# A MetaFormer block on one core: the whole convolution stage in 64x64 tensor tiles, in two rounds over pairs of PSUM banks

## The chip, the core and the metric

The kernel runs on one core of one Trainium2 chip. The metric is the device time of one execution in microseconds (us). The kernel before was run three times: 953.1, 950.99 and 952.64 us, median 952.64. One further execution was taken by the hardware profiler. PE is TensorE (the matrix engine; PEld are its weight loads), DVE is VectorE, ACT is ScalarE, POOL is GpSimd, SP is SyncE, which issues most transfers here.

## What is computed

The input is `x` of shape 4 x 32 x 128 x 128 in float32: 4 batches and 32 tokens (channels), each an image of 128 x 128. Two layers follow one another:

```python
x = x + _L0_conv_ref(_ln_c(x), ...)      # spectral attention and mixers
t = x as tokens; t = t + _L0_ffn_ref(_ln_t(t), W, V, gamma, beta)
x = x + _L1_conv_ref(_ln_c(x), bias, up_filter, dn_filter)
t = x as tokens; t = t + _L1_ffn_ref(_ln_t(t), W, V, gamma, beta)
```

`_ln_c` and `_ln_t` normalise each row of 128 numbers. The part that concerns us is the second convolution and the two neighbours of it:

```python
def _L1_conv_ref(x, bias, up_filter, dn_filter):
    x = x + bias                                    # one number per token
    x = repeat(repeat(x, 2, axis=2), 2, axis=3)     # 128x128 -> 256x256
    x = _conv_same(x, up_filter)                    # 12x12, separable
    x = leaky_relu(x, 0.2) * sqrt(2)
    x = _conv_same(x, dn_filter)                    # 12x12, separable
    return x[:, :, ::2, ::2]                        # back to 128x128

def _L1_ffn_ref(x, W, V, gamma, beta):
    Wx = einsum('bti,hi->bth', x, W)                # product of the features
    Wx = batch-normalised over all rows, times gamma plus beta
    y_t = sigmoid(wx_t + y_{t-1} @ V.T)             # a scan over tokens and rows
    return ys
```

The scan runs over all tokens and rows, `32 * 128` steps in sequence for each batch.

## The kernel before, in words

The whole activation, `XA` (128 partitions, 4 batches, 32 tokens, 128 columns), stays in SBUF. The program has these stages: the attention (to about 235 us in the profile), the mixers, whose order of work is the hand-set list `MIXERS` (to about 487 us), the first scan (to 547 us), **the convolution stage (547 to 869 us)**, and the second scan with the output (869 us to the end). The scans take all tokens and batches side by side, in four pieces of 32 rows each, which start from a guess with 12 rows of run-up and are checked at the end; `WX` holds the products before a scan and the states after it. If a check fails, a slow sequential program would run after it; it does not here.

The convolution stage is one function body, `parallel()`, from line 1980 on. Its order of work is the list `CONVOLUTIONS` (lines 54 to 117), some 1,500 pieces that a planner wrote out beforehand. `in_order` (line 499) ties the instructions of PE, DVE, ACT, POOL and, in this stage, SP to the order in which the pieces are issued, so each engine does its share of the list strictly in sequence. A piece is a letter code and a number: a token `t` (0 to 31) or a unit `u` (0 to 63; one unit is one token and two of its four batches). For one token the pieces are:

- `Y t` (lines 1961 and 2057): four 128x128 transposes on PE turn the states of the first scan back to rows, into a PSUM tile `ps_y`; `A t` (line 2060) adds them to `XA` on DVE.
- `CS`, `CN`, `CP`, `CO`: row statistics of the sum (DVE, line 383), means and variances by seven small DVE operations (lines 370 and 2004), the power -1/2 on POOL (line 2016), shifts on DVE (line 2019). Groups of one to four tokens share them.
- `X t.b` (line 2065): the normalised image `XN` of one batch. For b = 3 ACT makes it, else POOL; the first two tokens use DVE and ACT.
- `Ra u`, `Rb u` (line 2101): the row half of the upsampling filter, two batches, as matmuls with 64 rows and 128 columns of weights and 134 moving columns; `Q u` (line 2118) copies the result to `q1` on ACT.
- `Ka u`, `Kb u` (line 2123): the column half, the same tile shape, into two single-bank PSUM tiles.
- `La`, `Lb` (line 2141): ACT writes `above = relu(0.8 x)` from PSUM; `Va`, `Vb` (line 2147): DVE writes `U = 0.2 x + above`, reading the same PSUM bank and `above`.
- `Da v`, `Db v` (line 2155): both halves of the downsampling filter, of unit `v` and of unit `v - 1`, as 64x64 matmuls with 67 moving columns; `C`, `E` copy the results on ACT, `AD` adds to `XA` on DVE.
- `FS`, `FN`, `FP`, `FO`, `N`: the statistics of the result, and the normalised features `xn` (two batches on POOL, two on ACT); `FS` also issues from SP the transfer of the token's rows to DRAM.
- `T t` (line 427): four 128x128 transposes; `TC` copies them on ACT; `M t` (line 441): one 128x128 matmul over 512 columns; `PS` (DVE) takes its statistics and `PC` (ACT) puts it into `WX`.

A float32 matmul appears in the profile as two matmuls and two weight loads, a transpose as one of each.

[...]two row tiles with different data can run side by side[...]. That is why `R`, `K` and `D` come in two rounds, a and b: in round a the upper row tile writes the bank of batch 0 and the lower one that of batch 1, in round b they change places and add to what is there. Round b may begin only when round a is through, which the program ensures by an empty instruction on SP that waits for round a and for which round b waits (lines 2045 to 2055). Before, those empty instructions wait for the first matmul of each tile in round a by their code.

[...]Before, the pool `ps_t` (line 1873) has four single-bank buffers that `Y`, `K`, `T`, `M`, and later the output share; the pool `ps_c1` (line 1984) has two banks for `R` and two for `D`.

Of the kernel before, what the change touches and what calls it, by code (L numbers as in the profile page):

```python
# [54 lines left out]
Y0 Y2 A0 Y1 A2 Y3 Y4 CS0 Y5 A1 CN0 Y6 CS1 CP0 CS2 CO0 CN1 X0.0 CP1 A3 X0.1 X0.3 X0.2 Ra0 CS3 Y7 Rb0 CO1 A4 Q0 X1.0  # L55
Ra1 CN2 X1.3 Y8 X1.1 X1.2 Rb1 CP2 CS4 Q1 A6 Ra2 A5 Rb2 CO2 Ka0 CS5 X2.0 X3.0 Kb0 X2.3 CS6 X2.2 X3.3 X3.2 Q2 CK X2.1
Lb0 Ra3 X3.1 La0 Rb3 Va0 A7 Vb0 Y9 CS7 Da0 A8 Db0 CN3 C0 Ka1 CS8 Y10 CP3 Kb1 A10 La1 A9 Lb1 Va1 Q3 Y11 CS9 Ra5 Y14
CO3 Rb5 Vb1 X4.0 A11 X4.3 X4.1 Da1 X4.2 CS10 Ka2 CS11 Db1 A14 Kb2 C1 CN4 La2 Ka3 E0 Va2 Lb2 CP4 Kb3 Q5 AD0 Y12 Vb2
La3 Ra4 A12 Da2 Lb3 Va3 Rb4 CS12 Db2 Q4 X5.0 X5.3 X5.2 CO4 Ka4 C2 X5.1 Ra6 Vb3 Kb4 E1 CS14 Ka5 La4 Da3 Lb4 AD1 Va4
Rb6 FS0 Db3 Vb4 Kb5 C3 Y15 La5 Y13 E2 A15 Q6 Da4 Va5 Lb5 Ra7 AD2 Db4 Vb5 A13 Ka6 C4 CS15 Rb7 E3 Kb6 X8.0 Q7 AD3 Da5  # L60
La6 X8.2 CS13 X8.1 Lb6 Ka7 Va6 X8.3 Ra8 Db5 FS1 Kb7 C5 Vb6 Rb8 La7 CN5 Y16 E4 Y19 Lb7 Va7 CP5 Da6 Q8 AD4 Vb7 Ra9 Db6
A16 A19 Ka8 C6 Rb9 CS16 E5 Kb8 X6.0 Q9 CO5 Da7 X6.2 X6.3 AD5 X6.1 La8 Ra10 CS19 Ka9 Lb8 Db7 Va8 FS2 Kb9 C7 Rb10 La9
Vb8 Y17 E6 Va9 Q10 Da8 Lb9 AD6 A17 Ka10 Db8 Vb9 CS17 Kb10 C8 Ra11 La10 Y18 E7 Va10 Rb11 Lb10 Da9 X7.0 Q11 AD7 Vb10
X7.1 X7.3 Ka11 X7.2 FS3 Ra12 Db9 A18 Rb12 C9 FN0 Kb11 Q12 Y20 CS18 FP0 E8 La11 Ra13 Da10 AD8 Lb11 Va11 Rb13 A20 Ka12
Q13 Vb11 Db10 CN6 Kb12 C10 FO0 Ka13 CS20 CP6 La12 Ra14 E9 Kb13 Va12 Lb12 Da11 AD9 La13 Vb12 Rb14 FS4 Db11 Q14 Lb13
N1.0 CO6 Ka14 C11 N0.0 Ra15 Va13 N1.1 N1.2 Kb14 E10 N0.1 Rb15 Vb13 La14 Da12 Q15 AD10 Lb14 Ka15 N1.3 Db12 N0.3 N0.2
Ra16 Va14 C12 Kb15 E11 T0 Vb14 La15 Da13 AD11 TC0 FS5 Lb15 Rb16 Db13 Q16 Ra17 C13 Va15 T1 E12 Vb15 Rb17 N2.0 TC1
Da14 X9.0 AD12 Q17 X10.0 X9.3 Ka16 X9.1 N2.2 Ka17 X10.1 X10.3 Kb16 X9.2 N2.3 Db14 La16 X11.0 X10.2 Lb16 Ra18 Va16
X11.1 Kb17 C14 X11.2 X11.3 M0 Vb16 N2.1 E13 La17 N3.0 AD13 Da15 Lb17 PS0 N3.1 N3.3 FS6 Rb18 N3.2 Db15 Q18 PC0 T2
Va17 C15 Ra19 Vb17 M1 TC2 E14 AD14 Da16 PC1 PS1 Ka18 Db16 Kb18 C16 Rb19 La18 M2 X12.0 E15 Va18 Q19 X12.1 Da17 Lb18  # L70
X12.2 AD15 PS2 X12.3 Ka19 Vb18 Ra20 PC2 Kb19 FS7 Db17 La19 Lb19 FN1 Rb20 C17 T3 Va19 FP1 Q20 Y21 E16 Vb19 Ra21 TC3
Da18 AD16 A21 Ka20 CS21 Db18 FO1 Kb20 C18 N4.0 Rb21 N5.0 La20 M3 X13.0 E17 Va20 Lb20 N4.1 Da19 Q21 X13.2 AD17 Vb20
X13.3 X13.1 Ka21 N4.3 N5.1 FS8 Ra22 N4.2 Kb21 PC3 Db19 La21 PS3 Lb21 Rb22 Va21 C19 T4 Y22 Q22 Vb21 N7.0 Y24 E18 N7.1
TC4 A22 Da20 N5.3 AD18 N5.2 CS22 Ka22 N7.2 Ra23 N7.3 A24 Kb22 Db20 La22 CS24 Lb22 Rb23 Va22 C20 T5 X14.0 Q23 M4 Vb22
N6.0 E19 X14.2 TC5 AD19 Da21 X14.1 N6.2 PS4 N6.1 N6.3 Ka23 FS9 X14.3 Ra24 PC4 Kb23 Db21 La23 Lb23 Rb24 Va23 C21 T6
Q24 M5 Vb23 E20 TC6 AD20 Da22 PC5 Ka24 PS5 Ra25 Db22 Kb24 C22 Rb25 La24 M6 X15.0 E21 Va24 Q25 X15.1 Da23 Lb24 X15.2
AD21 PS6 X15.3 Ka25 Vb24 Ra26 PC6 Db23 FS10 Kb25 C23 Rb26 La25 T7 E22 Y23 Va25 Q26 Da24 Lb25 AD22 A23 TC7 Ra27 Vb25
Db24 CS23 Ka26 C24 Rb27 CN7 E23 Kb26 X16.0 Q27 Da25 X16.1 AD23 La26 CP7 FS11 Lb26 Ka27 X16.3 Ra28 Va26 Db25 FN2 Kb27
C25 Vb26 Rb28 La27 M7 E24 FP2 CO7 Q28 Da26 Va27 Lb27 PC7 AD24 Ka28 Vb27 Ra29 Kb28 PS7 Rb29 La28 X16.2 Db26 FO2 Lb28
X17.0 Y25 Q29 N9.0 Va28 Y26 X17.2 C26 A25 X17.1 Ra30 X17.3 Vb28 Y27 N8.0 E25 N9.2 N9.1 Da27 AD25 N8.2 N8.1 A26 N9.3  # L80
Ka29 N8.3 FS12 Db27 CS25 Kb29 C27 A27 Rb30 La29 T9 CS26 E26 T8 Lb29 N10.0 Da28 TC9 N11.0 Va29 N10.1 TC8 AD26 N11.1
Db28 Vb29 Q30 N10.3 CS27 Ka30 C28 Ra31 N11.3 Kb30 CN8 E27 N11.2 Da29 AD27 CP8 La30 FS13 Lb30 M8 N10.2 Va30 Rb31 PC8
Db29 Vb30 Q31 PS8 C29 Ka31 X18.0 CO8 Ra32 E28 X18.1 Kb31 X18.3 AD28 X18.2 Da30 La31 Lb31 Va31 Rb32 Db30 Q32 Vb31
Ka32 C30 Ra33 E29 Kb32 AD29 Da31 La32 FS14 Lb32 Rb33 Va32 M9 Q33 X19.0 X19.3 X19.2 Vb32 Ka33 PC9 X19.1 Ra34 PS9 Db31
Kb33 C31 Rb34 La33 T10 E30 T11 Va33 Q34 Da32 TC10 AD30 Lb33 Ra35 TC11 Db32 Vb33 C32 Ka34 Rb35 E31 Kb34 X20.0 Q35
AD31 Da33 La34 X20.2 FS15 X20.1 Lb34 Ka35 Va34 X20.3 Ra36 Kb35 FN3 M10 La35 Vb34 FP3 Rb36 Lb35 PS10 Db33 Q36 PC10
Ra37 Va35 C33 M11 Vb35 E32 PC11 Da34 AD32 FO3 N12.0 PS11 Ka36 N13.0 N12.2 Db34 N12.1 N12.3 N13.1 N13.3 Kb36 C34 Rb37
La36 T12 X21.0 E33 Y28 Va36 N14.0 X21.3 Da35 X21.2 Q37 AD33 X21.1 TC12 A28 Ra38 N14.1 Lb36 FS16 M12 N14.3 N14.2 Vb36
Rb38 PC12 Db35 CS28 Q38 N13.2 Ka37 PS12 C35 Ra40 Kb37 E34 Ka38 La37 AD34 Da36 Lb37 Va37 Kb38 Vb37 Db36 La38 Lb38
Rb40 Va38 C36 T14 Q40 T13 Vb38 E35 N15.0 Ra39 TC13 AD35 Da37 N15.1 TC14 FS17 N15.2 Rb39 Ka40 N15.3 X22.0 Q39 Db37  # L90
X22.1 X22.3 X22.2 Ka39 C37 Ra41 E36 Kb39 AD36 Da38 La39 Lb39 Va39 Kb40 Db38 La40 Vb39 Rb41 C38 Va40 X23.0 Q41 M13
X23.2 E37 X23.3 X23.1 AD37 Lb40 Da39 PS13 Vb40 Ra42 PC13 Db39 FS18 Ka41 C39 Rb42 E38 Kb41 Q42 AD38 Da40 La41 Lb41
Ka42 Va41 Ra43 Kb42 Vb41 Db40 La42 Lb42 Rb43 Va42 C40 M14 X24.0 Q43 Vb42 X24.2 T15 E39 X24.1 PS14 X24.3 Da41 TC15
AD39 PC14 Ka43 FS19 Ra44 Kb43 FN4 Db41 Lb43 FP4 La43 Rb44 C41 M15 Va43 Q44 Y29 Vb43 E40 PC15 Da42 AD40 A29 Ka44 FO4
PS15 Ra45 N16.0 Kb44 N17.0 CS29 N16.2 Rb45 N16.1 La44 Db42 X25.0 Q45 N17.1 Y30 Va44 C42 X25.1 Ra46 X25.3 A30 X25.2
Ka45 E41 Lb44 AD41 Da43 N16.3 CS30 N17.2 Kb45 N17.3 Vb44 Db43 La45 FS20 Lb45 Rb46 T16 C43 Va45 T17 Q46 N18.0 Vb45
Y31 E42 N19.0 TC16 Da44 AD42 N18.1 N19.2 A31 N19.1 N18.3 Ka46 TC17 CS31 Ra47 Kb46 N19.3 N18.2 Rb47 CN9 Db44 La46
X26.0 Lb46 CP9 M16 Va46 C44 Q47 Vb46 M17 E43 X26.3 PS16 Da45 PC17 AD43 PC16 FS21 Ra48 X26.1 Db45 X26.2 CO9 Rb48 C45
PS17 Ka47 Q48 T18 E44 Kb47 TC18 AD44 Da46 La47 Lb47 Va47 Ra49 Db46 Vb47 Ka48 C46 Rb49 E45 Kb48 X27.0 Q49 AD45 Da47
X27.2 La48 FS22 X27.1 X27.3 Ka49 Lb48 Va48 Ra50 Kb49 Vb48 Db47 La49 Lb49 Rb50 Va49 C47 M18 Q50 Vb49 T19 E46 PS18  # L100
Da48 TC19 AD46 PC18 Ka50 Ra51 Kb50 Db48 La50 Lb50 Rb51 Va50 C48 M19 X28.0 Q51 Vb50 X28.1 E47 X28.2 Ra52 PS19 X28.3
Da49 AD47 PC19 Rb52 FS23 Ka51 Q52 Db49 FN5 Kb51 C49 FP5 Ka52 La51 Ra53 E48 Kb52 Va51 Lb51 Da50 AD48 La52 Vb51 Rb53
# [172 lines left out]
def _network(  # L275
# [1585 lines left out]
    def parallel():  # L1861
# [20 lines left out]
        class Recurrence(Inputs):  # L1882
# [98 lines left out]
        with (  # L1981
# [75 lines left out]
            def state_rows(t):  # L2057
                ps_y[t] = f0.rows(t)
# [300 lines left out]
```

## Time and profile before

| what | value |
|---|---|
| median of three runs | 952.64 us (950.99 to 953.1) |
| the profiled execution | 953.73 us, of which the span is 951.6 us |
| PE busy, whole span | 846.8 us (89%) |
| DVE, ACT, POOL busy, whole span | 741.7, 662.7, 243.3 us |
| convolution stage, 547 to 869 us | 322.0 us |
| PE busy in it | 309.2 us, 8012 matmuls |
| DVE, ACT, POOL busy in it | 231.5, 227.9, 118.8 us |

The span runs from the first to the last instruction of the profile. The busy times of an engine are the union of its instructions, so neighbours that overlap in the pipeline count once. Matmul ends are modelled, so their starts are the better guide. In a group's line the first number is busy time, then the mean length of one instruction, then the idle time ahead of it and what ended that.

### The profile page before, as it was taken

The numbers are of one execution on the slowest core, as the hardware profiler recorded it, in microseconds if no ns is written. First come the engines' busy times: TensorE is split into PE (matmuls) and PEld (weight loads), VectorE is DVE, ScalarE is ACT, GpSimd is POOL, SyncE is SP. The second block draws the span as 40 slices with busy tenths as digits, with TensorE's granted clock in tenths as the row PEclk, the third lists the DMA queues.
The fourth block names the chain that finished last, engine by engine and source line by source line (L and its number), as shares of the span: only waits on it lengthen the run. The fifth ranks groups of instructions, "written<-read, shape, count | busy, mean of one in ns | idle before, by whom it ended". The sixth has DMA issues, their size and how long they took to land.

```text
span 951.6 us, 30245 instructions
## 1 busy us (share of the span) xinstructions
PE 846.8 (89%) x12310; PEld 620.9 (65%) x12310; DVE 741.7 (78%) x2381; ACT 662.7 (70%) x1640; POOL 243.3 (26%) x448
## 2 busy tenths in 40 slices
PE   2999979997897889997879969999999999997995
PEld 2666556677565555644357857888787888775884
DVE  5997477876668899899888888967676576667997
ACT  2775546667745878989778824687777777776773
POOL 2000000020244545355310033443353244131000
PEclk9999979996777999999999969999999999998998
DMA  9905000000101111120000000110110101117443
GB/s 227 222 4 118 1 1 1 1 1 1 46 23 31 39 46 46 46 68 26 20 1 1 1 1 14 38 37 26 37 37 26 37 26 37 37 38 265 162 165 133
DMA packets 69013, 49.60 MB, mean 52 GB/s; under 512 B 4417, under 2 KB 63809, under 8 KB 68801
## 3 DMA queue, kind: packets, MB, share of 16 engines
q1 hardware_dynamic: 68529, 47.31, 17.3%
q8 instruction: 99, 1.62, 0.7%
q0 software_dynamic: 288, 0.01, 0.2%
q10 hardware_dynamic: 48, 0.26, 0.2%
q14 instruction: 49, 0.40, 0.1%
HBM read 30.68 MB, written 16.88 MB: 50 GB/s over the span
## 4 chain that ended last, share of the span: by engine, by line
PE 55%; DVE 23%; ACT 6%; issue 2%; POOL 2%; DVEq 0%; ACTq 0%; SPq 0%; POOLq 0%
PE ps_dn L2162 11%; PE ps_up L2131 8%; PE ps_scan L1911 8%; PE ps_up L2108 4%; DVE XA L1582 4%; PE ps_wx L444 3%; DVE XA L1581 3%; PE ps_y L1301 3%; PE pm L1053 2%; PE ps_inv L479 2%; PE ps_st L1424 2%; DVE ps_scan L1912 2%; PE ps_xt L430 2%; DVE bn L447 2%; PE ps_out L2230 1%
## 5 line engine op out<-in xcount | busy, mean ns | idle before, releaser
L2151 DVE SCALAR_TENSOR_TENSOR U<-ps_up,above 128x512 f32<-128x512 f32 x128 | 85.0, 685 | 51.9 <-ACT above L2144 33.1
L1912 DVE SCALAR_TENSOR_TENSOR ps_scan<-WXY,bs,ps_scan 128x128 f32<-128x128 f32 x352 | 102.2, 361 | 11.3 <-PE ps_scan L1911 9.5
L2162 PE MATMUL ps_dn<-WXY,U 64*64 64x67 f32 x4096 | 90.6, 226 | 1.0 <-ACT p L2191 0.5
L2131 PE MATMUL ps_up<-WXY,q 64*128 64x134 f32 x1024 | 91.1, 299 | 0.4
L2162 PEld LDWEIGHTS ps_dn<-WXY,U 64*64 64x64 f32 x4096 | 72.5, 134 | 28.3 <-ACT p L2191 10.4
L2144 ACT ACTIVATE above<-ps_up 128x512 f32<-128x512 f32 x128 | 73.3, 602 | 20.9 <-PE ps_up L2131 19.1
L444 PE MATMUL ps_wx<-xt,wvt 128*128 128x512 f32 x128 | 70.5, 637 | 6.5 <-ACT WXY L451 4.5
L2131 PEld LDWEIGHTS ps_up<-WXY,q 64*128 64x128 f32 x1024 | 68.7, 189 | 9.3 <-ACT q L2121 1.2
L2036 POOL TENSOR_SCALAR XN<-XA,c_r,c_o 128x128 f32<-128x128 f32 x90 | 42.9, 487 | 99.7 <-PE ps_up L2108 71.1
L2187 ACT COPY q<-ps_dn 128x512 f32<-128x512 f32 x64 | 37.7, 589 | 44.0 <-PE ps_dn L2162 43.8
L2108 PE MATMUL ps_up<-WXY,XN 64*128 64x134 f32 x512 | 60.3, 313 | 6.9 <-DVE XN L2036 3.4
L848 PE MATMUL ps_st<-cst,XA 128*128 128x130 f32 x256 | 43.4, 309 | 14.8 <-ACT XA L831 11.6
L1639 ACT ACTIVATE xn<-XA,f_o,f_r 128x128 f32<-128x128 f32 x120 | 50.9, 489 | 4.7 <-DVE f_o L1621 4.6
L447 DVE BATCH_NORM_STATS2 bn<-ps_wx 128x6 f32<-128x512 f32 x64 | 44.2, 694 | 12.2 <-ACT WXY L451 8.2
L1418 ACT ACTIVATE Z<-Z,k,aB 128x128 f32<-128x128 f32 x128 | 51.0, 480 | 3.4 <-DVE Z L1413 3.2
L848 PEld LDWEIGHTS ps_st<-cst,XA 128*128 128x128 f32 x256 | 35.1, 205 | 27.9 <-ACT XA L831 12.7
L2162 PE MATMUL ps_dn<-WXY,q 64*64 64x67 f32 x2048 | 53.0, 218 | 0.0
L2108 PEld LDWEIGHTS ps_up<-WXY,XN 64*128 64x128 f32 x512 | 40.5, 192 | 18.2 <-issue 5.4
L1581 DVE SCALAR_TENSOR_TENSOR XA<-ps_inv,r1B,xin 128x128 f32<-128x128 f32 x128 | 44.1, 345 | 8.7 <-PE ps_inv L1574 8.7
L1582 DVE SCALAR_TENSOR_TENSOR XA<-Z,gB,XA 128x128 f32<-128x128 f32 x128 | 46.5, 363 | 5.0
L451 ACT COPY WXY<-ps_wx 128x512 f32<-128x512 f32 x60 | 35.0, 587 | 21.9 <-DVE bn L447 16.8
L430 PEld LDWEIGHTS ps_xt<-ident,xn 128*128 128x128 f32 x256 | 28.7, 142 | 29.6 <-ACT xt L438 7.5
(443 smaller groups left out, 2155.9 us busy)
## 6 DMA issues: line engine op xcount, KB each, us to landing
XA<-in_x_dram SPq DMA_DIRECT2D x16, 512.0 KB, 7.3
xin<-in_x_dram SPq DMA_DIRECT2D x32, 256.0 KB, 3.2
turned<-XA SPq DMA_DIRECT2D x32, 256.0 KB, 2.3
XA<-turned SPq DMA_DIRECT2D x8, 1024.0 KB, 14.4
out_dram<-res SPq DMA_DIRECT2D x64, 128.0 KB, 2.1
WXY<-dd SPq DMA_DIRECT2D x4, 544.0 KB, 11.1
WXY<-md SPq DMA_DIRECT2D x4, 144.0 KB, 5.5
WXY<-m1d SPq DMA_DIRECT2D x1, 544.0 KB, 11.5
```

Source lines behind the costliest of these rows:

```text
L444: mm(self.held[t], self.t[:, 0, :], xt, start=True, stop=True)
L447: nc.vector.bn_stats(self.stats[:, t, :], self.held[t].rearrange("p b w -> p (b w)"))
L848: mm(p[:, i, :], XA[:, b, t0 + j + i, :], cst[:, C_E : C_E + 130], start=True, stop=True)
L1581: stt(a, p2[c, b][:, i], r1B[:, j : j + 1], xin[c, b - b % 2][:, b % 2, i], ALU.mult, ALU.add)
L1582: stt(a, Z[c][:, b, i], gB[c][:, n : n + 1], a, ALU.mult, ALU.add)
L1911: mm(p4, self.t[:, 1, :], prev, start=True, stop=True)
L1912: stt(p4, WX[:, :, h, :], s[:, 0:1], p4, ALU.mult, ALU.add)
L2108: i = mm(dst[:, :, reach[k]], XN[u // 2][h, u % 2 * H2 + b, :], UR[h, :, reach[k]], start=(n == 0), stop=(n == 1), skip_group_check=True)
L2131: i = mm(dst[:, r, :, reach[k]], q1[u][w, b, r * P : r * P + P], UC[w, :, reach[k]], start=(n == 0 and r == 0), stop=(n == 1), skip_group_ ...
L2144: nc.scalar.activation(above[u, k], pu[u][k], AF.Relu, scale=1.0 - SLOPE)
L2151: stt(U[u][:, k].rearrange("p r s m -> p (r s m)"), pu[u][k], SLOPE, above.pop((u, k)), ALU.mult, ALU.add)
L2162: i = mm(dst, data, taps, start=(n == 0 and (k, j) in new), stop=(n == 1), skip_group_check=True)
```

## The change

All PE work of the convolution stage is written as 64x64 tiles, four at a time, in two rounds over a pair of banks by one helper, `in_rounds`. `Y` and `T` become matmuls against a 64x64 piece of the identity (so they have rounds a and b, and 16 matmuls of 64 columns instead of four transposes of 128), `M` becomes eight matmuls of 256 columns, `R` and `K` have twice as many matmuls, with 64 weight columns each; `D` keeps its matmuls. The empty SP instruction now waits for the last matmul of each tile in round a.

```diff
+            HALVES = slice(0, HALF), slice(HALF, P)
+            REACH = slice(P - E, P), slice(0, E)
+            TILES = [(i, j) for i in range(2) for j in range(2)]
...
+            def in_rounds(name, pool, products):
+                def piece(n):
+                    def run(u):
+                        if n == 0:
+                            banks[name, u] = pool.tile([P, 2, 4 * P], F32, tag="x", name=f"ps_{name}")
+                        last = {}
+                        for i, j, dst, data, taps in products(u, banks[name, u], n):
+                            m = mm(dst, data, taps, start=(n == 0 and (i, j) not in last), stop=(n == 1),
+                                   skip_group_check=True)
+                            if n == 1 and (i, j) not in last:
+                                after(m, ended[name, u])
+                            last[i, j] = m
+                        if n == 0:
+                            ended[name, u] = nc.sync.nop(nofuse=True)
+                            for m in last.values():
+                                after(ended[name, u], m)
+                    return run
+                return piece(0), piece(1)
...
+            def turned_by(source):
+                def products(t, p, n):
+                    for c in range(2):
+                        for i, j in TILES:
+                            b = i ^ n
+                            o = c * P + i * HALF
+                            yield (i, j, wide(p, b)[HALVES[j], o : o + HALF],
+                                   source(t, HALVES[i], 2 * b + c, HALVES[j]), ident[HALVES[i], HALVES[i]])
+                return products
...
+            def feature_products(t, p, n):
+                for i, j in TILES:
+                    b = i ^ n
+                    yield (i, j, wide(p, b)[HALVES[j]], f1.t[HALVES[i], 0, HALVES[j]],
+                           xt[t][HALVES[i], 2 * b : 2 * b + 2, :].rearrange("p b h -> p (b h)"))
...
+            def up_cols(u, p, n):
+                for r in range(2):
+                    for i, j in TILES:
+                        b = i ^ n
+                        o = r * P + j * HALF
+                        dst = p[:, b].rearrange("p (r s m) -> p r s m", r=2, s=2)
+                        yield (i, j, dst[HALVES[j], r, :, REACH[i]], q1[u][HALVES[i], b, o : o + HALF],
+                               UC[HALVES[i], :, REACH[i]])
```

The leaky ReLU changes sides. ACT now copies the raw sum out of PSUM, and DVE works from SBUF alone:

```diff
-                    above[u, k] = cv.tile([P, 4 * P], F32, tag="above", name="above")
-                    nc.scalar.activation(above[u, k], pu[u][k], AF.Relu, scale=1.0 - SLOPE)
+                    raw[u, k] = cv.tile([P, 4 * P], F32, tag="raw", name="raw")
+                    nc.scalar.copy(raw[u, k], banks["k", u][:, k])
...
-                    stt(U[u][:, k].rearrange("p r s m -> p (r s m)"), pu[u][k], SLOPE, above.pop((u, k)),
-                        ALU.mult, ALU.add)
+                    v = raw.pop((u, k))
+                    stt(U[u][:, k].rearrange("p r s m -> p (r s m)"), v, SLOPE, v, ALU.mult, ALU.max)
```

POOL takes over the image of batch 3 of the convolution's input and of batch 2 of the features from ACT, and the means take six small DVE operations instead of seven:

```diff
-                normalise(("DVE", "ACT", "DVE", "ACT")[b] if t < 2 else "ACT" if b == 3 else "POOL",
+                normalise(("DVE", "ACT", "DVE", "ACT")[b] if t < 2 else "POOL",
...
-                normalise(("DVE", "DVE", "ACT", "ACT")[b] if t >= NT - 2 else "POOL" if b < 2 else "ACT",
+                normalise(("DVE", "DVE", "ACT", "ACT")[b] if t >= NT - 2 else "POOL" if b < 3 else "ACT",
```

The PSUM pools are cut anew: two banks that `R` and `T` share, two for `D`, and two pairs for `Y`, `M` and `K`. `ps_t` is opened only for the output, with two buffers instead of four, and the weights of the second FFN are turned in a pool of their own between the first scan and the stage, no longer ahead of the scan:

```diff
-        ps_t = ctx.enter_context(tc.tile_pool(name="ps_t", bufs=4, space=PSUM))
...
-        f1 = Recurrence(1, xtp, wk, ps_t, ps_t, ("t", "t"))
-        f1.prepare()
+        with tc.tile_pool(name="ps_f", bufs=1, space=PSUM) as ps_f:
+            f1 = Recurrence(1, xtp, wk, ps_f, ps_f)
+            f1.prepare()
...
-            tc.tile_pool(name="ps_c1", bufs=1, space=PSUM) as ps_c1,
+            tc.tile_pool(name="ps_r", bufs=1, space=PSUM) as ps_r,
+            tc.tile_pool(name="ps_d", bufs=1, space=PSUM) as ps_d,
+            tc.tile_pool(name="ps_k", bufs=2, space=PSUM) as ps_k,
...
-        with tc.tile_pool(name="outp", bufs=3) as outp:
+        with (
+            tc.tile_pool(name="outp", bufs=3) as outp,
+            tc.tile_pool(name="ps_t", bufs=2, space=PSUM) as ps_t,
+        ):
```

Last, the list `CONVOLUTIONS` is written anew for these pieces. A stretch of it, before and after:

```diff
-Q24 M5 Vb23 E20 TC6 AD20 Da22 PC5 Ka24 PS5 Ra25 Db22 Kb24 C22 Rb25 La24 M6 X15.0 E21 Va24 Q25 X15.1 Da23 Lb24 X15.2
...
+Ka24 N7.0 TC4 Db22 Vb23 N7.1 N7.3 Ra25 N7.2 C22 Ma4 Rb25 E21 Kb24 X15.0 Q25 AD21 Da23 Lb24 X15.2 FS10 Mb4 X15.1 La24
```

In the new order 235 of the 289 pairs of rounds have more than one short pass of PE work between a and b, 41 have one short pass (one round of `R`, `T` or `Y`) and 13 have none. Outside this stage the instructions of every engine stand in the same order as before.

## Prediction

> **What bounds the kernel now.** I read the chain of work that ended last first: PE holds over half of it, and its largest lines are the convolution stage's.
>
> ```profile
> PE 55%; DVE 23%; ACT 6%; issue 2%; POOL 2%; DVEq 0%; ACTq 0%; SPq 0%; POOLq 0%
> ```
>
> Then the busy time of each engine by windows, over the whole stage and in parts (the columns are window, length, PE, weight loads, DVE, ACT, POOL with counts, PE clock, DMA share, GB/s).
>
> ```profile
> 547.00:570.00 23.00, 15.64 (x95) 11.46 (x95) 19.97 (x81) 6.42 (x15) 7.72 (x9) 0.70 0.00 1
> 570.00:590.00 20.00, 18.55 (x452) 15.53 (x456) 18.56 (x72) 8.94 (x18) 8.49 (x8) 0.92 0.01 3
> ...
> 715.00:734.00 19.00, 19.00 (x474) 14.52 (x478) 11.90 (x35) 15.78 (x34) 8.61 (x13) 1.00 0.10 28
> ...
> 547.00:869.00 322.00, 309.24 (x8012) 247.17 (x8010) 231.54 (x723) 227.85 (x486) 118.76 (x170) 0.97 0.12 35
> ```
>
> From 590 us on PE is never idle; in the first 43 us DVE is nearly full and PE waits for it. So the stage is PE's, with a head that is DVE's. Busy is not yet useful; what PE's time goes into, its timeline tells (start, length, line, count).
>
> ```profile
> 700.57 0.41 PE L2162 MATMUL ps_dn<-WXY,q 64*64 64x67 f32 x16
> 700.91 0.73 PE L2131 MATMUL ps_up<-WXY,q 64*128 64x134 f32 x8
> 701.48 0.39 PE L2108 MATMUL ps_up<-WXY,XN 64*128 64x134 f32 x4
> 701.74 0.73 PE L2131 MATMUL ps_up<-WXY,q 64*128 64x134 f32 x8
> 702.40 0.70 PE L2162 MATMUL ps_dn<-WXY,U 64*64 64x67 f32 x32
> 702.92 0.41 PE L2162 MATMUL ps_dn<-WXY,q 64*64 64x67 f32 x16
> 703.26 1.12 PE L444 MATMUL ps_wx<-xt,wvt 128*128 128x512 f32 x2
> 704.32 0.50 PE L2108 MATMUL ps_up<-WXY,XN 64*128 64x134 f32 x4
> ```
>
> The single records that these lines merge start in steady groups: four 64x64 tiles of 67 columns every 58.4 ns, two 64x128 tiles of 134 columns every 114.2, one 512-column matmul 429 before its successor. That is one law: 0.833 ns per column plus 2.5, whatever the tile, for as many tiles as run together. Now the borders. From the last start of a group to the first of the next it is 148 ns after 67-column tiles, 204 after 134 columns, 523 after 512: 90 to 94 more than the pace. And the first group then needs 109 instead of 58 (64x64) or 219 instead of 114 (64x128), because its weight loads (51 or 105 ns) lie open. At borders where the shape stays (`K` to `R`, where no round is waited for) neither is seen: 107 ns, the pace. So a change of tile shape costs 141 to 195 ns, and I count 326 of them in the stage.
>
> [...] The trace shows it at the addition of line 2196, which has two SBUF inputs:
>
> ```profile
> L2196 DVE TENSOR_TENSOR XA<-XA,p x64: 401/425/634, 582.8 to 859.2; 128x256 f32<-128x256 f32 x64
> ```
>
> ```profile
> 656.12 0.45 POOL L2036 TENSOR_SCALAR xn<-XA,f_r,f_o 128x128 f32<-128x128 f32 x1
> 656.55 1.04 POOL L2036 TENSOR_SCALAR XN<-XA,c_r,c_o 128x128 f32<-128x128 f32 x2
> 656.63 0.63 DVE L2196 TENSOR_TENSOR XA<-XA,p 128x256 f32<-128x256 f32 x1
> ```
>
> It normally takes 425 ns; started just after a POOL image it takes 634, and the second POOL image then takes 610 instead of 448. [...]
>
> **The change, part by part.** *PE streaming.* By the law above, before and after:
> - `D`: 6144 matmuls in 1536 fours at 58.4: 89.7 us, both.
> - `K`: 512 pairs at 114.2: 58.5; after, 2048 matmuls in 512 fours: 58.5.
> - `R`: 256 pairs, 29.2; after, 256 fours, 29.2. Twice the instructions, the same streaming.
> - `M`: 64 x 429 plus 32 open loads of 105: 30.8; after, 128 fours of 256 columns at 215.8: 27.6.
> - `T` and `Y`: 256 transposes at 109: 28.1; after, 2048 matmuls of 64 columns in 512 fours at 55.8: 28.6.
>
> Sum 236.3 before, 233.6 after. So streaming gains almost nothing; the gain is the other 309.2 - 236.3 = 72.9 us. Of it the 326 changes of shape are about 55 us (0.17 each); the rest is the slow clock of the head and second rounds that were waited for. After, no shape changes inside the stage.
>
> *Waits between rounds.* A second round follows the last matmul start of the first by at least 375 ns where nothing lies between (`K` at 582.04 us), through SP's empty instruction; 701.74 is such a hop already[...]. That the code now names the last matmul costs nothing new. One short pass between covers 56 to 114 + 223 to 232 ns, [...]: 41 x 0.1 = 4.1; 13 without cover at 0.34 are 4.4. I take 8 us. Behind that wait stand all later matmuls of PE; behind SP's empty instructions stand the transfers of rows to DRAM, and those wait for DVE. In the stage SP waited for DVE 5 us in all, which work in between hid; taken at nothing, up to 10.
>
> *DVE.* 128 leaky operations from two SBUF inputs at 693 instead of 685 ns: +1.0. One small operation less in 20 groups at 0.175: -3.5. Turned weights moved into the head: +0.4. 231.5 becomes 229. New waits for POOL: 192 operations with two SBUF inputs (128 of `V`, 64 of `AD`); the observed block is 634 - 425 = 0.21, so at most 40 us, at least 0. POOL reads for 210 images x 0.45 = 94 us of some 265; a start in the blocking part (about 0.28 of each) meets 22%, with half to full block, 6 to 9 us. I take 8: 237. Its cover is PE's 242; were PE faster, this would be bare.
>
> *ACT.* Copy for relu, 602 against 595 ns: 0. 60 images leave at 29.2/64 = 0.46: -27, so about 200. *POOL* gets them at 0.45: 146, plus up to 60 x 0.3 of waits for `V`. Both have room: the window 715 to 734 has ACT at 83%.
>
> *PSUM.* `D` keeps one pair: two rounds (1.4 us), one or two passes between (0.5), copies of 589 and 383 ns with their hops (1.2) make 3.1, against about 3.9 per unit. `R` and `T` share a pair three times a token: 3 x 1.7 of 7.8. The bank of `K` is freed by ACT alone. No stall taken. The output's two buffers are refilled every 2.2 us by PE and emptied in 0.71 by DVE: nothing.
>
> *The head.* DVE does before the first `D` one `A`, two `CS`, the scan's check and small operations less (0.6 + 1.7 + 2.8 + 0.5): 23 becomes 17.3 us, in which PE has 7.3 us of work; 10 us idle, and 2 more until PE leads. The tail keeps its 3 idle us.
>
> *The sum.* 233.6 + 8 + 10 + 2 + 3, and 9 more (4%) because DVE at 237 and PE at 242 take turns in being late, which neither did before: 266 us for 322, a gain of 56. The profiled execution, 953.73 us, would take 897.7; its span is 951.6, the 2.1 around it stay. It lies 1.1 above the median, so the median becomes 896.6: I say **897**.
>
> **The rivals.** *DVE takes the stage* because `V` and POOL's 60 extra images shut each other out. For it: 634. Against: only 4 of 64 `AD` met it. At 40 us DVE has 269, plus 3 + 9 + 3 as above: 284, so 915. *The rounds are bare*: SP's empty instructions come late and half of the 289 pairs stall 0.2: +29, 924. *It becomes slower*: PE isn't fed. The stage would issue 23,552 PE instructions instead of 16,022, 89 per us; the densest 20 us before had 61 per us (1223 from 600 to 620), although one round of `D` did 96 in 0.86 us. If the supply held 61, 386 + 13 us: 1030; it is slower than before from about 76 per us downward. Against it: PE's instruction queue moved 1.62 MB in 99 packets over the whole span and took 0.7% of the engines. *The change doesn't do what it says*: four wide tiles don't run side by side. `D` shows four at the same column rate, so this has little.
>
> **How the numbers follow.** Forecast, 880 to 905: 0.62. DVE and POOL, 905 to 925: 0.18. Bare rounds, 910 to 940: 0.12. Better than 880 (no hops, no taking turns: -17): 0.03. Unfed PE, above 955: 0.05. The range 879 to 920 leaves out the last two and half of the third, near 0.2 with the edges. About 0.2% is what a measurement of this kernel can tell from no change. Faster 0.94, same 0.01, slower 0.05.
>
> **What would show it.** Right: PE matmuls of 64x64 alone in the stage, fours of 134 columns 114 ns apart, PE's busy time near 245 us, the stage near 266. DVE right: `V` with a median near 693 and a tail near 900. Wrong: `V`'s mean above 850, PE idle with the wait for SP's empty instruction or for ACT's copies above 20 us, or gaps of PE that nothing released.

## The result, and the profile after

The changed kernel takes 998.26 us (996.77 to 1002.19, four runs) against 952.87 us for the kernel before on the same chip: the ratio is 1.048, interval 1.045 to 1.052. It is slower by 45 us where 56 us less was forecast, as the third rival had it.

The profiled execution has a span of 997.6 us for 951.6, 46 us more. First the chain of work that ended last, of the kernel after:

```profile
PE 53%; DVE 19%; issue 8%; ACT 5%; POOL 2%; SPq 1%; DMA 0%; DVEq 0%; ACTq 0%; POOLq 0%
```

"issue" is time in which an engine waited for nothing that the profile shows. It was 2% before and is 8% now. 6% of the span is 60 us, more than the whole loss.

Then the windows of the same stage (window, length, PE, weight loads, DVE, ACT, POOL with counts, PE clock, DMA share, GB/s):

```profile
547.00:914.00 367.00, 290.84 (x11801) 261.19 (x11799) 232.67 (x713) 210.20 (x435) 164.10 (x230) 0.99 0.13 37
547.00:570.00 23.00, 18.80 (x475) 16.13 (x477) 19.64 (x81) 9.90 (x26) 8.68 (x11) 0.93 0.01 3
570.00:590.00 20.00, 16.69 (x673) 15.62 (x669) 14.57 (x45) 9.93 (x22) 7.05 (x8) 0.91 0.06 18
600.00:620.00 20.00, 15.75 (x685) 14.44 (x688) 15.03 (x53) 10.46 (x22) 7.26 (x5) 1.00 0.11 30
715.00:734.00 19.00, 15.39 (x651) 14.22 (x639) 11.44 (x28) 11.40 (x25) 5.83 (x11) 1.00 0.11 32
```

Before, PE was busy for all of the 19 us from 715 on; now it stands still for about a fifth of each of these windows, from 600 us on at full clock, and in those from 570 us on no other engine is above 80%. PE has less work (291 us instead of 309) in a longer stage (368 instead of 322). So no engine is full. The waits of the kernel after say what PE waited for (engine, tile, line, releaser: us in total, times, longest):

```profile
PEld ps_d L2061 <- issue: 36.7, 43, 1.8
...
PE ps_d L2061 <- issue: 29.7, 38, 1.7
```

And PE's timeline from 600 us on, only the lines that begin after a stop:

```profile
600.72 0.62 PE L2061 MATMUL ps_d<-WXY,U 64*64 64x67 f32 x26 [0.88 <-issue]
...
604.44 0.33 PE L2061 MATMUL ps_k<-WXY,q 64*64 64x134 f32 x2 [1.03 <-issue]
...
607.88 0.56 PE L2061 MATMUL ps_k<-WXY,q 64*64 64x134 f32 x10 [0.38 <-issue]
...
611.52 0.40 PE L2061 MATMUL ps_d<-WXY,U 64*64 64x67 f32 x11 [0.66 <-issue]
...
615.33 0.57 PE L2061 MATMUL ps_k<-WXY,q 64*64 64x134 f32 x11 [0.64 <-issue]
```

The stops come every 3.4 to 3.8 us, whatever piece is due, in the middle of a pass (one round of a piece) too. That is a beat of its own. The line of PE's instruction queue on the page after tells whose:

```profile
q8 instruction: 128, 2.10, 0.9%
```

Before it was 99 packets and 1.62 MB. A packet is 16 KB (1.62 MB in 99, 2.10 MB in 128). PE's matmul and load records rose by 7,552 (the 23,552 of the prediction less 16,000), the packets by 29, so one packet carries about 260 instructions. I set PE's records and these packets side by side in the trace, and call it a stop where more than 0.3 us lie between the starts of one matmul and the next. Of the 104 stops between 560 and 910 us 84 end 2.0 to 2.8 us after the start of a packet, where some 20 would by chance, and 84 lie within four neighbouring places when PE's instructions are counted by 256. The packets themselves follow each other at 3.74 us in the median and never below 3.24.

*Theory.* PE's instructions are fetched in packets of 256, and the next packet can't be there earlier than about 3.5 us after the last (a round figure between the 3.24 and the 3.74). That is 73 instructions per us. I call this the supply. Where 256 instructions hold less than 3.5 us of work, PE stands still for the rest. *Rivals:* the stops come from the waits between the rounds, the new order or the new pools; or VectorE and GpSimd shut each other out and PE's stops follow from that; or it is simply PE's own work, with the turns of states (`Y`) at fault.

### The profile page after: what moved, and what is told of

Its sections match the earlier page's. It is cut to its first block, busy times and chain, and to the rows that moved or that the text cites. A ratio compares the mean times of both kernels' runs of the same rounds, so it can differ in the third digit from the quotient of the medians.

```text
span 997.6 us, 37888 instructions
## 1 busy us (share of the span) xinstructions
PE 830.5 (83%) x16086; PEld 634.9 (64%) x16086; DVE 741.6 (74%) x2361; ACT 644.8 (65%) x1580; POOL 288.9 (29%) x508
## 4 chain that ended last, share of the span: by engine, by line
PE 53%; DVE 19%; issue 8%; ACT 5%; POOL 2%; SPq 1%; DMA 0%; DVEq 0%; ACTq 0%; POOLq 0%
PE ps_d L2061 10%; PE ps_scan L1915 8%; PE ps_k L2061 6%; DVE XA L1587 4%; DVE XA L1586 3%; PE ps_r L2061 3%; PE ps_w L2061 3%; PE ps_y L2061 3%; PE ps_y L1306 2%; PE pm L1058 2%; PE ps_st L1429 2%; PE ps_x L2061 2%; PE ps_inv L484 2%; PE ps_out L2242 1%; DVE ps_scan L1916 1%
## 5 line engine op out<-in xcount | busy, mean ns | idle before, releaser
L2061 PE MATMUL ps_d<-WXY,U 64*64 64x67 f32 x4096 | 102.8, 222 | 20.5 <-issue 19.9
L2168 DVE SCALAR_TENSOR_TENSOR U<-raw 128x512 f32<-128x512 f32 x128 | 86.5, 697 | 33.4 <-ACT raw L2160 28.8
L2061 PEld LDWEIGHTS ps_d<-WXY,U 64*64 64x64 f32 x4096 | 91.4, 134 | 26.6 <-issue 24.5
L2061 PE MATMUL ps_k<-WXY,q 64*64 64x134 f32 x2048 | 96.4, 279 | 12.8 <-issue 11.9
L2160 ACT COPY raw<-ps_k 128x512 f32<-128x512 f32 x128 | 70.0, 594 | 35.0 <-PE ps_k L2061 34.4
L2061 PEld LDWEIGHTS ps_k<-WXY,q 64*64 64x64 f32 x2048 | 70.1, 134 | 18.8 <-issue 15.2
L2061 PE MATMUL ps_d<-WXY,q 64*64 64x67 f32 x2048 | 64.7, 220 | 9.8 <-issue 9.8
L2061 PE MATMUL ps_r<-WXY,XN 64*64 64x134 f32 x1024 | 65.6, 281 | 5.1 <-issue 3.2
L2040 POOL TENSOR_SCALAR xn<-XA,f_r,f_o 128x128 f32<-128x128 f32 x90 | 48.8, 551 | 72.0 <-PE ps_x L2061 55.4
L2199 DVE TENSOR_TENSOR XA<-XA,p 128x256 f32<-128x256 f32 x64 | 27.9, 436 | 48.3 <-ACT p L2194 48.1
L2061 PEld LDWEIGHTS ps_d<-WXY,q 64*64 64x64 f32 x2048 | 52.3, 134 | 12.2 <-issue 12.2
```

Source lines behind the costliest of these rows:

```text
L2040: e.tensor_scalar(dst, src_, r, o, ALU.mult, ALU.add)
L2061: m = mm(dst, data, taps, start=(n == 0 and (i, j) not in last), stop=(n == 1), skip_group_check=True)
L2160: nc.scalar.copy(raw[u, k], banks["k", u][:, k])
L2168: stt(U[u][:, k].rearrange("p r s m -> p (r s m)"), v, SLOPE, v, ALU.mult, ALU.max)
```

## The experiments

For times of the stage I take each profiled span less 629.6 us, which is what the kernel before has outside the stage (951.6 - 322). That counts in what differs outside it. Between the last matmul of the first scan and the last product `M` the trace has 319.8 us before and 361.8 after, so 42 of the 46 us lie inside; for the other kernels the two measures agree within 3 us, but for one that is named below. The first four kernels below were run once each.

### The supply by itself

The kernel does nothing of the reference's computation. It runs eight sections like this one (the loop is shortened here), with the columns, shapes and weights that the expectation lists:

```python
for c in range(128):
    for i in range(2):
        for j in range(2):
            nc.tensor.matmul(p[H[j], i, :n], S[H[i], (2 * c + i) % 32, H[j]], SF[H[i], 4096 : 4096 + n], start=True, stop=True, ...)
```

> This kernel does none of the reference's computation: it copies data through SBUF and then runs eight sections of TensorE matmuls, 128 groups each of tiles that run side by side, with nothing else at work. Supply theory (TensorE's instructions arrive in pieces of 256, and a piece can't come faster than about every 3.5 us, as the changed kernel's trace shows): fours of 64x64 tiles with 32, 67 and 100 columns all take about 3.5 us per 256 instructions (28 us for a section of 2048), 134 columns 3.65 (29 us), 256 columns 6.9 (55 us). Rival (the gaps of TensorE come from waits inside the convolution stage, and TensorE is not limited by its instructions): the law of 0.833 ns per column plus 2.5 holds throughout, 1.87 us per 256 instructions at 67 columns (15 us a section), 2.75 at 100 (22 us), 3.65 at 134, 6.9 at 256, and at most 1.75 at 32. Fours of 64 columns whose weights are read with a stride: 115 to 123 ns each as in the changed kernel (15.5 us a section), unless the supply makes it 28. Pairs of 64x128 tiles (1024 instructions a section): 134 columns 114 ns (14.6 us); 67 columns between 58 ns (7.4 us, if loads of two tiles hide) and 105 ns (13.4 us, if the load of 128 columns sets the pace).

Its page, busy times and the instruction queue:

```profile
PE 248.1 (74%) x7168; PEld 244.8 (73%) x7168; DVE 1.3 (0%) x8; POOL 0.2 (0%) x4
...
q8 instruction: 56, 0.92, 1.1%
```

7168 matmuls and 7168 loads in 56 packets: 256 in each, exactly. Its timeline in the section with 67 columns:

```profile
81.72 2.09 PE L2308 MATMUL ps<-S 64*64 64x67 f32 x128 [1.27 <-issue]
...
85.72 2.10 PE L2308 MATMUL ps<-S 64*64 64x67 f32 x128 [1.91 <-issue]
...
89.45 2.09 PE L2308 MATMUL ps<-S 64*64 64x67 f32 x128 [1.63 <-issue]
...
92.90 2.09 PE L2308 MATMUL ps<-S 64*64 64x67 f32 x128 [1.36 <-issue]
```

Here the beat lies bare. PE does exactly 128 matmuls (with their 128 loads, one packet) in 2.1 us, stands still for 1.3 to 1.9 us, and begins again 3.45 to 4.0 us after the last time. Nothing else runs. By groups of one shape (busy time, mean of one, idle before it):

```profile
L2308 PE MATMUL ps<-S 64*64 64x256 f32 x1024 | 55.5, 376 | 0.0
...
L2308 PE MATMUL ps<-S 64*64 64x134 f32 x1024 | 29.8, 274 | 0.0
...
L2308 PE MATMUL ps<-S 64*64 64x100 f32 x1024 | 23.9, 247 | 4.7 <-issue 4.7
L2308 PE MATMUL ps<-S 64*64 64x67 f32 x1024 | 19.4, 239 | 81.4 <-DMA S<-out_dram 72.3 <-issue 9.2
```

From first to last start the sections took 28.3 us with 67 columns, 28.3 with 100, 29.6 with 134 and 55.2 with 256. Per packet of 256 that is 3.54, 3.53, 3.69 and 6.89 us. So 67 and 100 columns cost the same; from 134 columns on, where a packet holds 3.65 us of work, the stops vanish and the law of the prediction holds to 1%. The rival's 15 us is refuted. Fours of 64 columns with strided weights ran at 146 ns each, 37.0 us a section, with no stop: that is a second thing (below), and more than the 115 to 123 ns expected. Pairs of 64x128 tiles ran at 114 ns with 134 columns and at 112 with 67, near the 105 of one open load. A section has 256 such fours or pairs, since each of its 128 groups of float32 matmuls stands twice in the trace (256 matmuls as x512 in a section of pairs); the expectation's section times for these last three kinds reckon with 128 and are half of what its own paces give.

### More work for the same instructions, and fewer instructions

The first kernel lets the downsampling taps run over all columns, the added ones being zeros; the second leaves out the odd rows of the doubled image, so its result is another one:

```diff
-dst[HALVES[j], s, REACH[i]], U[v][...], DR[HALVES[i], r, REACH[i]]      # and the same for DC
+dst[HALVES[j], s, :],        U[v][...], DR[HALVES[i], r, :]
```

> The changed kernel with the moving taps of the downsampling filter widened from 67 to all 128 columns (the added columns hold zeros): the same number of TensorE instructions, but 1536 fours at 109 instead of 58 ns, 78 us more streaming. Supply theory: streaming was 251 us over 92 pieces of 256 instructions, 2.7 us each, under the 3.5 that a piece needs; with 78 us more it is 3.6, so most of the addition falls into time in which TensorE stood idle: stage 377 to 402 us instead of 367, span 1008 to 1033 us. Rival (TensorE's own work and the waits between rounds set the stage): the addition counts in full, stage about 445, span about 1075 us.

```diff
-                    for r in range(2):
+                    for r in range(1):
```

> The changed kernel with half of the row half of the downsampling filter left out (the odd rows of the doubled image are not used): 4096 TensorE instructions less, 16 pieces of 256, and 30 us less streaming. Supply theory: 16 pieces at 3.5 to 3.8 us, 56 to 61 us: stage 306 to 311, span 936 to 942 us. Rival (TensorE's own work sets the stage): 30 us, stage 337, span 967. Rival (DVE, ACT or POOL set it): stage within 5 us of 367, span above 990.

The windows of the stage, of the kernel with wide taps and then of the one with half the rows:

```profile
547.00:918.00 371.00, 351.96 (x11781) 329.19 (x11782) 231.38 (x701) 207.90 (x423) 162.58 (x230) 0.99 0.13 37
```

```profile
547.00:855.00 308.00, 258.19 (x9737) 227.70 (x9737) 229.68 (x705) 204.93 (x426) 173.56 (x230) 0.99 0.15 44
```

With wide taps PE is busy 61 us longer, and the stage is 4 us longer (372 us, span 1001.7; 7 us between its own ends): of 78 us of work nearly all went into time in which PE stood still anyway. That is even less than the theory's own 10 to 35. With 4096 instructions less the stage is 59 us shorter (308.5, span 938.1), with 30 us of work gone: as the theory has it, and 29 us more than PE's work alone can explain. Work hardly counts and instructions do. Longer passes could also have covered waits between rounds, but those come to some 10 us in all in the kernel after, and the section with 67 columns, which has no rounds, stops at the same beat.

### The other engines

```diff
-nc.scalar.copy(raw[u, k], banks["k", u][:, k])
+nc.scalar.activation(raw[u, k], banks["k", u][:, k], AF.Relu, scale=1.0 - SLOPE)
-stt(U[u][:, k]..., v, SLOPE, v, ALU.mult, ALU.max)
+stt(U[u][:, k]..., banks["k", u][:, k], SLOPE, v, ALU.mult, ALU.add)
-[b] if t < 2 else "POOL",
+[b] if t < 2 else "ACT" if b == 3 else "POOL",       # and xn: b < 2 instead of b < 3 on POOL
```

> The changed kernel with the engines' shares of the kernel before: the leaky operation again from PSUM and a relu by ScalarE, and 60 images back from GpSimd to ScalarE. TensorE's instructions are the same. Supply theory: stage within 5 us of 367, span 992 to 1003. Rival (VectorE's operations with two SBUF inputs and GpSimd's added images block each other, and TensorE's idle time is a consequence): the stage falls by 15 us or more, span below 983.

Groups of GpSimd, of the kernel after (as on its page) and of this one:

```profile
L2040 POOL TENSOR_SCALAR XN<-XA,c_r,c_o 128x128 f32<-128x128 f32 x120 | 66.3, 565 | 23.6 <-PE ps_r L2061 14.8
```

```profile
L2040 POOL TENSOR_SCALAR XN<-XA,c_r,c_o 128x128 f32<-128x128 f32 x90 | 40.8, 465 | 55.0 <-PE ps_r L2061 24.2 <-DVE c_o L2031 10.2 <-ACT p L2194 5.7
```

The images are shorter again, 465 instead of 565 ns, which fits VectorE and GpSimd having hindered each other; but the stage is 372 us, span 1001.4. It changes nothing at the end. This rival falls.

### Fewer instructions by whole tiles, in the new order

In three kernels some of the new pieces are made whole again, at the place of their round a:

```diff
+def whole_turned(source):
+    def products(t, p):
+        o = both(p)
+        for b in range(NB):
+            nc.tensor.transpose(o[:, b * P : b * P + P], source(t, b), ident)
...
+def whole_product(t, p):
+    for b in range(2):
+        mm(wide(p, b), f1.t[:, 0, :], xt[t][:, 2 * b : 2 * b + 2, :]...)
```

> The changed kernel with its order and its pools, but the turn of the states, the turn of the features and their product again in whole 128x128 tiles (the product as two matmuls of 256 columns): 19,200 TensorE instructions in the stage instead of 23,552, 75 pieces of 256 instead of 92, and up to 192 changes of tile shape at 0.17 us come back, 32 us; streaming stays near 236. Supply theory: 75 pieces at 3.5 to 3.8 us are 262 to 285 us, the work of TensorE is 236 + 32 + 8 = 276, and the two don't add up but take turns: stage 290 to 305 us, span 920 to 936, so faster than both kernels. Rival (TensorE's idle time of the changed kernel has to do with its order, its pools or its waits between rounds): the stage stays above 345 us and the span above 975.

> As the kernel with three whole pieces, but the product of the features stays in 64x64 tiles: 20,096 instructions in the stage, 78.5 pieces, and 128 changes of shape, 22 us. Supply theory: 78.5 pieces at 3.5 to 3.8 us, 275 to 298; work 234 + 22 + 8 = 264: stage 292 to 308 us, span 922 to 939. Rival (order, pools or waits): above 345, span above 975.

> The changed kernel with only the turn of the states in whole 128x128 tiles: 21,760 instructions, 85 pieces, 64 changes of shape, 11 us; its fours with strided weights, 123 instead of 58 ns, are gone. Supply theory: 85 pieces at 3.6 to 3.8 us, 306 to 323 us, with the slow head stage 320 to 335, span 950 to 966. Rival (the strided loads of these fours are what costs): their 17 us and no more, less 11 for the changes of shape: stage about 360, span about 990.

The other side is the kernel before, with only the upsampling filter in 64x64 tiles:

```diff
-i = mm(dst[:, r, :, reach[k]], q1[u][w, b, r * P : r * P + P], UC[w, :, reach[k]], ...)
+for j, m in enumerate(rows_of_half):          # the same for the row half
+    i = mm(dst[m, r, :, reach[k]], q1[u][w, b, r * P + j * HALF : r * P + j * HALF + HALF], UC[w, :, reach[k]], ...)
```

> The kernel before, with its own order, pools, whole turns and products, and only the upsampling filter's two halves cut into 64x64 tiles: 19,072 instructions instead of 16,000 in the stage, and about 206 of 326 changes of tile shape are gone, 35 us. Both theories agree that the changes of shape cost 141 to 195 ns each: stage 287 us by that alone. Supply theory: 74.5 pieces at 3.5 to 3.8 us are 261 to 283 and lie close under that, so a part of the gain is lost in dense stretches: stage 290 to 306 us, span 920 to 936. If the supply did not matter: 283 to 289. If changes of shape cost nothing: 322, or more by the denser supply.

Measured, as ratios to the kernel before: 0.994 (0.992 to 0.996) with `Y`, `T`, `M` whole, 1.002 (1.000 to 1.003) with `Y`, `T` whole, 1.026 (1.023 to 1.029) with `Y` whole, and 1.002 (1.000 to 1.003) for the kernel before with 64x64 upsampling. Spans 943.5, 952.5, 970.9 and 956.6; the third is of the fastest of four executions, the last of the slowest of twelve. (With `Y` and `T` whole it is 19,968 instructions, not the 20,096 of the expectation.) Among the three in the new order fewer instructions are faster each time, in spite of more changes of shape, and their rivals (spans above 975, or about 990) are refuted; but all four came out above my expectation, by 5 to 21 us. I had put the head and the waits, which the kernel before has too, at 8 us. The kernel before has 34 of them: 322 less the 288 that the stepping below gives for its matmuls and changes of shape.

The last of the four was a disappointment of a different kind: by the list of pieces some 206 changes of shape are gone, and 35 us should have come of it. (In the kernel after, which cuts `R`, `K` and `D` in the same tiles, the next of them begins 18 to 51 ns after the last matmul start of the one before, by medians; in the kernel before it was 148 or 204 where their shapes change.) Its stage, and its waits:

```profile
547.00:874.00 327.00, 291.70 (x9574) 232.19 (x9573) 234.87 (x736) 229.13 (x499) 117.88 (x170) 0.97 0.12 35
```

```profile
PEld ps_dn L2165 <- issue: 16.3, 28, 1.3
...
PE ps_dn L2165 <- issue: 11.3, 18, 1.2
```

PE's busy time fell by 17.5 us, and it stood still for longer instead. This is the kernel for which the two measures of the stage differ: between its own ends the stage takes 320.3 us, as before, and some 4 us of the profiled loss arose ahead of it, where the first scan ended at 551.5 us instead of 547.1. From 590 us on, stops above 0.3 us that end 2.0 to 2.8 us after the start of a packet sum to 30 us, in the kernel before to 6. So the supply took back some 24 of the 35 us, by this estimate, in which a part of the stops stands by chance. The rest wasn't taken apart. Taken alone this run doesn't refute its third case, that changes of shape cost nothing, for that gave 322 us too. Against it stands the next kernel: it differs from the one with `Y`, `T`, `M` whole only in the tiles of `R` and `K`, and with 184 more changes of shape, but 3,072 fewer instructions, its stage is some 10 us longer.

### The order and the pools, with the old tiles

```diff
-for i, j in TILES:                                       # R; the same for K
-    yield (i, j, dst[HALVES[j], :, REACH[i]], XN[...][HALVES[i], ..., HALVES[j]], UR[HALVES[i], :, REACH[i]])
+for i in range(2):
+    yield (i, 0, dst[:, :, REACH[i]], XN[...][HALVES[i], ..., :], UR[HALVES[i], :, REACH[i]])
```

> The changed kernel's order, pools, leaky operation and shares of the engines, but all tile shapes of the kernel before: whole turns and products, 64x128 pairs for the upsampling filter, 64x64 fours for the downsampling one. 16,128 TensorE instructions in the stage, 63 pieces of 256, which at 3.5 us are 220 us and bind nowhere for long; by the list of pieces 344 changes of shape, 58 us, beside 232 of streaming and 8 of waits: 298, as in the kernel before (326 changes). Supply theory: like the kernel before or a little better, since the two kernels that share a tiling but not the order (1.0018 and 0.9943) differ by 7 us for the new order: stage 315 to 325, span 943 to 955. Rival (the new order, pools or shares cost something of their own, beside the tiling): stage above 335, span above 964.

Ratio 1.003 (1.002 to 1.005), span 954.4, stage 325. The new order, pools, leaky operation and shares together cost 3 us, by the interval 5 at most. The loss is in the tiles.

### The best version, and one that gained nothing

```diff
-    for b in range(2):
-        mm(wide(p, b), f1.t[:, 0, :], xt[t][:, 2 * b : 2 * b + 2, :]..., start=True, stop=True)
+    mm(p[:, 0], f1.t[:, 0, :], xt[t].rearrange("p b h -> p (b h)"), start=True, stop=True)
```

> The kernel with three whole pieces, with the product of the features as one matmul of 512 columns in one bank instead of two of 256: 128 TensorE instructions less in the stage, half a piece, and no second load. Supply theory: 0 to 4 us less than the 947 of that kernel, 943 to 947, ratio to the kernel before 0.990 to 0.995. Rival (the bank that the product now holds whole delays the next filter half): slower than that kernel by up to 5 us.

Ratio 0.990 (0.987 to 0.992), 942.3 us: faster than the kernel before by 1.0% and than the one after by 5.6%. Its stage, for comparison with the first window above:

```profile
547.00:857.00 310.00, 286.76 (x9544) 225.99 (x9543) 231.38 (x704) 203.97 (x426) 176.05 (x230) 0.99 0.13 38
```

PE is busy 92% of it, for 79% after. In the last kernel 16 of its 96 whole pieces were moved:

```diff
+LATE = {"y": (16, 17, 18, 27, 28), "x": (0, 6, 8, 12, 13, 15, 27), "w": (3, 20, 21, 24)}
...
+def early(u):
+    if u not in LATE[name]:
+        first(u)
+def later(u):
+    if u in LATE[name]:
+        first(u)
-return first, lambda u: None
+return early, later
```

> The kernel with whole pieces and the product in one bank, with 16 of its 96 whole pieces (5 turns of states, 7 turns of features, 4 products) made a few passes later, at the place of their former second round, where another whole piece or a dense stretch stands next to them. The same 19,072 instructions; by the list of pieces, 138 changes of tile shape instead of 160, 3.7 us; a stepping through the list with 3.5 us for each 256 instructions and 0.17 for each change gives 275.5 instead of 280.9 us. If supply and changes of shape together set TensorE's time: 3 to 6 us less than 942, 936 to 940, ratio 0.982 to 0.988. If the later turns make ScalarE and VectorE late instead: 942 or more.

Ratio 0.989 (0.985 to 0.993), 942.4 us: no gain, a miss. PE's stops above 0.5 us that end 2.0 to 2.8 us after the start of a packet went from 14 to 17 us. That fits a gain of 3.7 us in changes of shape that the supply took back, but the difference is too small to settle it; a late ScalarE isn't excluded.

### One stepping for all

Afterwards I stepped through each kernel's list of passes: the streaming times of the prediction (the fours of `Y` at 123 ns, see below), 0.17 us per change of shape, and at every 256th instruction a stop until 3.5 us have gone since the last such place. To each sum I added the same 34 us of head and waits, set so that the kernel before comes to its 322.

| kernel | instructions | stepping without supply | with supply | stage measured |
|---|---|---|---|---|
| after | 23,552 | 285 | 358 | 368 |
| after, wide taps | 23,552 | 363 | 369 | 372 |
| after, half of the rows | 19,456 | 255 | 302 | 309 |
| after, `Y` whole | 21,760 | 276 | 335 | 341 |
| after, `Y`, `T` whole | 19,968 | 286 | 320 | 323 |
| after, `Y`, `T`, `M` whole | 19,200 | 294 | 316 | 314 |
| before, upsampling 64x64 | 19,072 | 287 | 316 | 327 |
| new order, old tiles | 16,128 | 325 | 326 | 325 |

With the 3.5 us taken from the traces, eight stages come out within 11 us; without it five miss by 37 to 83. For the last two kernels the stepping gave 280.9 and 275.5 us beforehand, so 315 and 310 with the 34, and both measured 309.

## Why the prediction was wrong, point by point

- *PE bounds the stage, 236 us of streaming, 55 us in changes of shape.* Right as measured: in the kernel after, where all pieces have one tile shape, fours of 134 columns take 114 ns and of 256 columns 216 in the median, and the 148 or 204 ns at the borders are gone (above). With the upsampling in 64x64 tiles the kernel before had PE busy for 291.7 us of its stage instead of 309.2. But the time was not free to be gained: by the stepping above, which is an estimate, the changes of shape were also pauses in which instructions came in.
- *Streaming 233.6 after.* Right for `R`, `K`, `D`, `M` and `T`; the term `T` and `Y`, 28.6, was mis-sized. The fours of `T` took 59 ns in the median, those of `Y` 123, 17 us more. Both read 64 columns; but `Y` loads weights from `WX`, where neighbouring columns lie 32 numbers apart. That the loads of both would hide behind the streaming was my estimate. An open load of 64 columns that lie side by side took 51 ns in the kernel before (a four of `D` 109 instead of 58); with a stride, the sections measured by themselves ran at 146 ns a four. The two groups of the kernel after, which have the same shape:

```profile
L2061 PE MATMUL ps_y<-ident,WXY 64*64 64x64 f32 x1024 | 45.9, 282 | 8.9 <-issue 6.0 <-DVE XA L2090 2.2 <-ACT WXY L1917 0.6
...
L2061 PE MATMUL ps_x<-ident,xn 64*64 64x64 f32 x1024 | 32.8, 220 | 6.6 <-issue 5.8 <-ACT xn L2037 0.5 <-ACT xt L2119 0.2
```

- *Waits between rounds, 8 us.* About right: PE's loads waited for SP's empty instruction some 10 us in `M`, `R` and `K` together. The 0.1 us for each of the 41 rounds with one short pass was an estimate.
- *DVE 237, of it 8 us for GpSimd.* The stage has 232.7. `V` took 697 ns on average (median 686, longest 859) for the 693 that line 1061 of the kernel before shows in the median for an addition of 512 numbers from two SBUF inputs, additions 436 on average for 433. It was GpSimd whose instructions grew: its images went from 487 and 477 to 565 and 551 ns, 16 us over 210 images, and taking that away again (465 ns with the old shares) didn't shorten the stage. That `V` would meet the same 0.21 us as the addition of line 2196 was an estimate; 8 of its 128 operations took over 750 ns.
- *ACT about 200, POOL 146 and up to 60 x 0.3 more.* 210 and 164.
- *The sum, 266.* Measured 368. Of the 102 us, stepping with and without supply puts 73 on the supply (324 less 251) and 17 on `Y`; the remaining 12 are head, waits and engines taking turns, and weren't taken apart. There are two small slips in the sums, on which nothing rests: by their own terms the 28.1 of `T` and `Y` before is 27.9, and the 924 of the bare rounds is 926.

The step that failed is the rejection of the rival "PE isn't fed", which left the sum without a term for the supply; by the stepping that term is 73 us, and the run with half the rows shows it directly: 4096 instructions less saved 29 us beyond their own work. The rival's own figure held: slower below about 76 instructions per us, and the supply gives 73. I gave it 0.05 for a reason that doesn't bear: the queue moved 1.62 MB and took 0.7% of the DMA engines. That is a share of bandwidth, and what bound was the time from one packet to the next: in the supply's own kernel the queue took 1.1% of the engines, each packet about 1.0 us, and still PE began on the next no sooner than 3.45 us after the last. In the kernel before, one packet follows another at 4.73 us on average, and none of 63 in the stage sooner than 3.4: had I set the 92 packets that the new stage needs against that shortest interval, 92 x 3.4 = 313 us, I would have had a figure 47 us above my sum. It would have been a warning and no proof, since the kernel before doesn't show that an interval can't be shorter. The second argument, a round of 96 instructions in 0.86 us, is less than one packet, so it can have come out of one that was already there. What I had named as the sign of error, "gaps of PE that nothing released", is what came.

## What to carry to other kernels

Cutting a matmul into more tiles that run side by side cost no streaming time here (134 columns took 114 ns as pairs of 64x128 and as fours of 64x64) but multiplied instructions (16,000 became 23,552). Before doing so, divide the new stage's PE instructions by 256 and hold the number of packets times the 3.5 us measured here against the work: 64x64 float32 tiles ran without stops at 134 columns (3.69 us per packet) and not at 100 (3.53 us, with 2.75 us of work by the law of the prediction). Ask of a queue how soon the next packet can come (here never sooner than 3.24 us in the kernel after), not only how busy it is (0.9%). And a pause that looks like waste (here the 141 to 195 ns of a change of shape) may be time in which something else catches up: of 35 us of such pauses that were taken out, some 24 came back as stops, by the estimate above.

## What the runs showed of the hardware

- PE's instructions came in packets of 256 (16 KB). In the kernel after, the next packet starts mostly 1.1 to 1.7 us after PE has taken up work again, takes about 1.1 us, and PE goes on some 2.4 us after its start: together 3.5 to 4.1 us. By themselves, with almost no other DMA traffic, it was 1.0 to 1.6 and 2.3 to 2.6 us, together 3.45 to 4.0. What makes up these times wasn't tried.
- Little of the supply was saved up: 4.2 us in which PE stood still between 547 and 570 us didn't prevent the stops from 600 us on, and the stage after, with 2.7 us of work per packet on average (251 us over 92 packets, `Y` at its 123 ns), ran at 3.9 (361.8 over 92). By itself, after 72 us without work, PE took 702 instructions before its first stop, and one packet arrived meanwhile: fewer than two packets had been at hand.
- Strided weights: fours of 64x64 tiles whose weight columns lie 32 to 64 numbers apart took 123 ns (`Y`, 32 apart) and 146 ns (by themselves, 64 apart), where those side by side took 59 (`T`).
- Open: fours of 32 columns ran evenly at 107 ns, 3.37 us per packet, almost without stops. That is the supply's pace, but the even spacing is unlike the other sections, and the cause wasn't tried.
